# Splitting the first of seven second-layer products in the 768-row parts of a one-core attention and mixture-of-experts kernel

## Chip, cores and metric

The kernel runs on one core of one Trainium2 chip. The metric is device microseconds (us) of one execution; lower is better. All arithmetic of the part in question is in 32-bit floats.

## What is computed

The block adds two things to its input `x` (8 sequences of 1024 tokens, 512 features): an attention layer on the normalised input, and then a mixture of 8 expert networks on the normalised sum. Each token goes to its two likeliest experts, with at most 160 tokens of each sequence per expert, so every expert has 1280 rows. The change touches only the second of the two matrix products of an expert:

```python
h = jax.nn.relu(jnp.einsum('enc,ech->enh', buf, W1) + b1[:, None, :])
y = jnp.einsum('enh,ehc->enc', h, W2) + b2[:, None, :]
```

`buf` holds the gathered rows (512 features), the hidden width is 2048, and `y` has 512 features again. The rows of `y` are multiplied by the probability of their expert and added into the output.

## The kernel before

**The order of the work.** Attention comes first; its last matmuls start at 1248 us. Then come 16 parts, two per expert: an even part of 768 rows (`nh = 3`) and an odd part of 512 rows (`nh = 2`). Each part runs a first layer (class `Hidden`, `layer1`, L1239 to L1321, matmuls at L1258) in eight steps, and then a second layer. The second layer of part 0 is `layer2` (L1361) alone. The seven later even parts go through `layer2_six` (L1545); the odd parts through `layer2_quad` (L1607). The kernel is recorded in a manual schedule: TensorE (PE), VectorE (DVE), ScalarE (ACT) and SyncE (SP) each execute their instructions in the order in which the program calls them. A generator called with `some(1, g)` places its next piece at that point of all the queues.

**Seven products.** Both layers are multiplied by a 2x2 block scheme with seven products in place of eight (Strassen's, in Winograd's form): sums of blocks of both operands are formed on DVE, seven block products run on PE, and further sums give the result. The hidden rows lie in a tile `hid` with seven operand blocks for each of eight column steps, `hid[:, q, k, :]`, for operands k = 0 to 6; the matching blocks of W2 and their sums are in `w2_tiles`. The second-layer product number n takes operand block and weight block as listed in `Second.OPERANDS` (L1444): product 5, for instance, takes operand block 4 and weight block 3.

**A 768-row part** has three blocks of 128 rows in each half. Blocks 0 and 1 are the pair; block 2 is the third block.

- The third block is a generator, `extra = layer2(i, 2, hid)` (L1549). Each of its seven products is eight matmuls of 128x128 by 256 columns (L1372). The first of them starts the accumulator `top`, copied to `y11` at L1384; the second accumulator `mid` comes with the next. Its pieces are placed between the products of the pair by `some(1, extra)`.
- For the pair, product 1 is plain: `pair_product` (L1536), sixteen matmuls of 256 columns (L1540) into one bank, copied to `y11` of both blocks by ACT at L1564.
- The other six products of the pair, in the order 5, 6, 2, 3, 7, 4, are themselves split by the same scheme (class `Second`). `both()` (L1474) puts eight DVE sums of 128x512 on the queue: four of weights (L1460) and four of rows (L1471), one of which is made in place, in `hid`. `run(c)` (L1482) issues seven chains of four matmuls of 128 columns (L1491) into three banks u, v and z, and six copies or sums that bring them to the four quarters of `c`:

```python
chain(u, a11, b11, True)
nc.scalar.copy(c11, u)
between()
chain(v, a21, t1, True)
nc.scalar.copy(c21, v)
chain(u, s2, t2, False)
```

Chain 1 needs no sums; chain 2 needs the first weight differences and the in-place row sum, chain 3 the third sums of both. Chain 3 adds into bank u, so it waits for the copy of c11 (L1500). After it come chains 4 to 7, a DVE sum into c11 (L1507), one into c22 (L1512) and one into c12 (L1513), and an ACT copy of c21 (L1515) that may only overwrite c21 once L1512 has read it.

- The sums need rooms. There are two sets of seven rooms (`sets`, L1555): `room`, made of the tiles `xe` and `xe_s` that the first layer is done with, and `other`, made of three `t1` tiles and the tile `xg`. Products take them in turn. The results go to three further rooms: `c5` for product 5 (and 4), `c6` for product 6, and `c` for all others in turn.
- `gate` (ACT, L1331) multiplies rows by their probability, `send` (POOL, an indirect DMA, L1336) adds them into the output. The y tiles come from a pool of five buffers (`yp`); a part uses six.
- `aside` is the preparation of the next part's rows: its first piece issues eight DMAs (`quarters`, SP, L1117) into `hid`, the columns of the pair's block 0 of operand 0; later pieces are DVE transposes (L1187) and sums (L1200 to L1203). SP's next issues are the loads of W1 (L1047).

Of the kernel before, what the change touches and what calls it, by code (L numbers as in the profile page):

```python
# [12 lines left out]
F32 = mybir.dt.float32  # L13
# [4 lines left out]
ALU = mybir.AluOpType  # L18
# [4 lines left out]
P = 128  # L23
# [51 lines left out]
def preln_attn_moe_kernel(  # L75
# [21 lines left out]
    nc = tc.nc  # L97
# [87 lines left out]
    t = xmp.tile([P, NTT, D], F32, name="x_mid").rearrange("p (i t) d -> p i (t d)", i=2)  # L185
    room = [t[:, i, :].rearrange("p (i s) -> p i s", i=2) for i in range(2)]
    for t in (base_first, room[0]):
        nc.gpsimd.iota(
            t, pattern=[[0, 2], [1, S]], base=0, channel_multiplier=0,
# [544 lines left out]
    def some(count, *gens):  # L734

        for gen in gens:
            while count and next(gen, 0) is None:
                count -= 1

    def rest(gen):  # L740
        got = None
        for got in gen:
            pass
        return got
# [283 lines left out]
    TT, STT = nc.vector.tensor_tensor, nc.vector.scalar_tensor_tensor  # L1028
# [3 lines left out]
    pools = {}  # L1032
# [89 lines left out]
    def new_xg():  # L1122
        return pools["gp"].tile([P, D], F32, name="xg", bufs=1)
# [233 lines left out]
    def new_y():  # L1357
        y = pools["yp"].tile([P, D], F32, name="y")
        return y, y[:, :DC], y[:, DC:]
# [79 lines left out]
    def split(t, part_of):  # L1439
        return [[part_of(t[:, 4 * k : 4 * k + 4], c) for c in range(2)] for k in range(2)]  # L1440

    class Second:

        OPERANDS = {2: (1, 1), 3: (2, 2), 4: (3, 6), 5: (4, 3), 6: (5, 4), 7: (6, 5)}  # L1444

        def __init__(self, i, hid, which, w_room, a_room):
            part, weight = self.OPERANDS[which]
            self.a = split(hid, lambda t, c: t[:, :, part, c * P : (c + 1) * P])
# [75 lines left out]
    two = range(2)  # L1524

    def as_pair(t):
        return t.rearrange("p (c n) -> p c n", n=P)

    def add_to(ys, parts):
        for b in two:  # L1530
            TT(as_pair(ys[b]), as_pair(ys[b]), parts[b], ALU.add)

    def of(ps, b):
        return ps[:, b * DC : (b + 1) * DC]

    def pair_product(i, hid, ps, part, weight, first, last, blocks=two):  # L1536
        ws = w2_tiles[chunks[i][0]]
        for b in blocks:
            for k in range(NHQ):
                nc.tensor.matmul(  # L1540
                    of(ps, b), lhsT=hid[:, k, part, b * P : (b + 1) * P], rhs=ws[weight][:, k, :],
                    start=first and k == 0, stop=last and k == NHQ - 1, skip_group_check=True,
                )

    def layer2_six(i, hid, aside, mix_next):  # L1545

        e = chunks[i][0]
        b2_b = b2_tiles[e]
        extra = layer2(i, 2, hid)  # L1549
        room = units(pools["xep"].tile([P, NCH, 2, HALF], F32, name="xe"), 6)  # L1550
        room += units(pools["xep"].tile([P, 3, 2, HALF], F32, name="xe_s"), 4)
        other = [
            u for _ in range(3) for u in units(pools["t1p"].tile([P, 4, 2, P], F32, name="t1"), 2)
        ] + units(new_xg(), 1)
        sets = [(room[:4], room[4:7]), (other[:4], other[4:7])]  # L1555
        c, c5, c6 = room[7:]
        second = {w: Second(i, hid, w, *sets[n % 2]) for n, w in enumerate((5, 6, 2, 3, 7, 4))}
        gate, send = zip(*(outputs(i, b) for b in two))
        second[5].both()
        top = pools["ps_p"].tile([P, 512], F32, name="ps_p")  # L1560
        y1, y11, y12 = zip(*(new_y() for _ in two))
        pair_product(i, hid, top, 0, 0, True, True)
        for b in two:
            nc.scalar.copy(y11[b], of(top, b))  # L1564
        second[6].both()
        five = second[5].run(c5)
        second[2].both()
        six = second[6].run(c6)
        for b in two:
            TT(six[b], six[b], as_pair(y11[b]), ALU.add)  # L1570
        TT(c5, c5, c6, ALU.add)
        some(1, extra)
        second[3].both()
        some(1, extra)
        add_to(y11, second[2].run(c))
        second[7].both()
        three = second[3].run(c)
        for b in two:
            TT(as_pair(y12[b]), five[b], three[b], ALU.add)
            TT(y1[b], y1[b], b2_b, ALU.add)  # L1580
        some(1, extra)
        for b in two:
            gate[b](0, y1[b])
            send[b](0, y1[b])
        second[4].both()
        some(1, extra)
        seven = second[7].run(c)
        y2, y21, y22 = zip(*(new_y() for _ in two))
        for b in two:
            TT(as_pair(y22[b]), five[b], seven[b], ALU.add)  # L1590
        TT(c6, c6, c, ALU.add)
        some(1, aside)
        four = second[4].run(c5, lambda: some(2, aside), lambda: some(1, aside))
        for b in two:
            TT(as_pair(y21[b]), six[b], four[b], ALU.add)
            TT(y2[b], y2[b], b2_b, ALU.add)
        some(1, aside)
        some(1, extra)
        for b in two:
            gate[b](1, y2[b])  # L1600
            send[b](1, y2[b])
        some(1, aside)
        some(1, extra)
        mix_next()
        rest(extra)
# [96 lines left out]
    def experts(ending):  # L1702
        pools["hp"] = to_end.pool("hp", 1, **right)
        pools["ps_tr"] = to_end.pool("ps_tr", 2, space=PSUM, reuse_waits="tile")
        pools["ps_p"] = to_end.pool("ps_p", 6, space=PSUM, reuse_waits="tile")
        box = first_parts
        mixes = loads = iter(())
        for i, (e, j0, nh) in enumerate(chunks):
            parts, box = box[0], [None]
            hid = pools["hp"].tile([P, NHQ, 7, HALF], F32, name="hid")  # L1710
            tiles, second, early_sums = None, None, iter(())
            if nh == 2:
                second = seconds(i, hid)
                early_sums = itertools.chain(second[0][5].weights(), second[0][2].weights())
            ahead = rows_ahead(i + 1) if i and i + 1 < len(chunks) else iter(())
            for q in range(NHQ):
                if i or q != NHQ - AHEAD - 1:
                    load_ahead(i * NHQ + q + AHEAD)
                some(3, loads)
                if q + 1 < NHQ:  # L1720
                    mix_w1(i, q + 1)
                if i and q > 1:
                    some(4 if q < 4 else 8, mixes)
                next(ahead, None)
                if 2 < q < 7:
                    some(2, early_sums)
                beside = [ending] if i or q < NHQ - 2 else [mixes] * (q + 3 - NHQ)
                tiles = layer1(Hidden(i, q, parts, hid, beside), tiles, q == NHQ - 1)
                if i == 0 and q == NHQ // 2:
                    rest(ending)  # L1730
                    to_router.close()
                    for name, bufs in (("w2p", 1), ("yp", 5), ("bp", 1)):
                        pools[name] = to_end.pool(name, bufs, reuse_waits="tile", **left)
                    load_ahead(NHQ - 1)
                    load_b2(0)
                    rest(load_w2(0))
                    mixes = mix_w2(0)
            rest(mixes)
            rest(ahead)
            room = [hid[:, 4 * h : 4 * h + 4, 0, :P] for h in range(2)] if i and nh > 2 else None  # L1740
            aside = start(gather(i + 1, room), box) if i + 1 < len(chunks) else iter(())
            if i == 0:

                aside = itertools.chain(behind(8, later_on(find_rows, 1)), aside)

            def mix_next():
                if i + 1 < len(chunks):
                    mix_w1(i + 1, 0)

            if i and nh > 2:  # L1750
                layer2_six(i, hid, aside, mix_next)
            elif i:
                layer2_quad(i, hid, second, aside, mix_next)
            else:
                for block in range(nh):
                    if block == nh - 1:
                        mix_next()
                    for _ in layer2(i, block, hid):
                        next(aside, None)
            rest(aside)  # L1760
            if i % 2 and e + 1 < E:
                load_b2(e + 1)
                loads = load_w2(e + 1)
                mixes = mix_w2(e + 1)
# [25 lines left out]
    for n in range(NCK):  # L1790
        more, late = n + 1 < NCK, last is not None
        b, c = divmod(n, NCH)
# [212 lines left out]
```

## Time and profile before

| what | us |
|---|---|
| median of 3 runs | 3158.21 (3156.91 to 3158.54) |
| the profiled execution | 3160.96 |
| its span, first to last instruction | 3159.2 |
| ACT busy in the span | 1686.1 (53%) |
| weight loads on PE busy in the span | 2149.6 (68%) |
| L1540 matmuls on PE, all parts (512 and 480 rows) | 113.4 and 106.0 |
| ACT copies at L1564 | 14, of 372 to 379 ns |

How to read it: the page gives for each engine the time in which it was busy, its share of the span and its number of instructions. The trace can be asked for the rows of one engine in a stretch of time; such a row gives the start in us from the start of the span, the length in us, the engine, the line of the kernel, the operation with output and input tiles, the shape and the number of equal instructions merged into it, and in brackets the idle time ahead of it with what ended it. Consecutive matmuls overlap at their ends, so the price of one is the distance from start to start, not its length. A 32-bit matmul of the program stands as two rows of the trace: the sixteen of `pair_product` are "x32". A further view gives the busy time of every engine and the granted TensorE clock in a stretch.

### The profile page before, as it was taken

What the parts mean: (1) busy time and instruction counts of PE and PEld (TensorE: products, weight loads), DVE (VectorE), ACT (ScalarE), POOL (GpSimd) and SP (SyncE); (2) the same over time, 40 slices, a digit from 0 to 9 for tenths busy, and PEclk for the clock granted to TensorE, in tenths of its full rate; (3) what the DMA queues carried; (4) which work ended last, traced back from release to release, by engine and by line L of the source; (5) the groups of instructions that cost most, each with busy time, mean ns of one, the idle gap of its engine ahead of it and who ended that gap; (6) DMA issues with size and microseconds to landing.
All of it is one profiled execution on the core that took longest, in us unless ns stands there. A gap on an engine that the chain in (4) does not pass through costs nothing.

```text
span 3159.2 us, 53457 instructions
## 1 busy us (share of the span) xinstructions
PE 3085.4 (98%) x20422; PEld 2149.6 (68%) x20422; DVE 2393.9 (76%) x4962; ACT 1686.1 (53%) x2672; POOL 421.3 (13%) x387
## 2 busy tenths in 40 slices
PE   5999999999999999999999999999999999999998
PEld 2454444544444544689699699699698698698697
DVE  8888888888888776738678678677777777777775
ACT  7888888888788885413423423423423423423423
POOL 3000202010101122320110110010110010110110
PEclk9999999999999999999999999999999999999999
DMA  5435454544545352433523523523523523423421
GB/s 168 148 101 167 110 165 133 156 135 147 155 140 161 81 168 63 142 84 96 156 52 92 156 50 99 155 50 99 150 54 102 142 57 105 135 57 108 133 46 22
DMA packets 288559, 358.86 MB, mean 114 GB/s; under 512 B 28376, under 2 KB 199088, under 8 KB 276272
## 3 DMA queue, kind: packets, MB, share of 16 engines
q1 hardware_dynamic: 264944, 312.20, 33.4%
q0 software_dynamic: 22912, 43.22, 7.5%
q8 instruction: 162, 2.65, 0.4%
q14 instruction: 93, 0.76, 0.1%
q10 hardware_dynamic: 448, 0.02, 0.0%
HBM read 207.02 MB, written 81.22 MB: 91 GB/s over the span
## 4 chain that ended last, share of the span: by engine, by line
PE 75%; ACT 12%; DVE 7%; DMA 3%; issue 2%; SPq 0%; POOLq 0%; POOL 0%; ACTq 0%; DVEq 0%
PE ps_p L1258 30%; PE ps_p L1491 13%; PE ps_s L688 8%; PE ps_p L1372 8%; PE ps_p L1540 7%; PE av L722 7%; ACT e L708 6%; ACT qk_c L598 1%; DMA xn_d<-xn 1%; ACT t_r L449 1%; PE ps_s L216 1%; ACT qk_r L449 1%; ACT L598 1%; DMA qk<-qk_r 1%; ACT L1908 1%
## 5 line engine op out<-in xcount | busy, mean ns | idle before, releaser
L688 PE MATMUL ps_s<-qk 64*128 64x512 f32 (+3 forms) x3072 | 584.6, 503 | 31.3 <-ACT e L708 13.7
L708 ACT ACTIVATE e<-ps_s 128x1024 f32<-128x1024 f32 (+1 forms) x640 | 554.4, 944 | 73.4 <-PE ps_s L702 45.3
L722 PE MATMUL av<-e,v 128*64 128x512 f32 (+3 forms) x3072 | 509.5, 488 | 0.0
L688 PEld LDWEIGHTS ps_s<-qk 64*128 64x128 f32 x3072 | 261.1, 188 | 219.1 <-ACT e L708 105.9
L722 PEld LDWEIGHTS av<-e,v 128*64 128x64 f32 x3072 | 206.0, 137 | 278.9 <-issue 258.5
L1258 PE MATMUL ps_p<-xe,w 128*128 128x256 f32 (+1 forms) x1024 | 317.6, 433 | 1.1 <-issue 1.1
L1258 PE MATMUL ps_p<-xe_s,t 128*128 128x256 f32 (+1 forms) x1024 | 317.7, 433 | 0.0
L1258 PE MATMUL ps_p<-xe,t 128*128 128x256 f32 (+1 forms) x1024 | 317.7, 433 | 0.0
L1336 POOL DMA_INDIRECT out_dram<-y,slots x80 | 127.6, 1595 | 1237.2 <-ACT y L1331 956.8
L773 POOL DMA_INDIRECT slot_d<-token,slot x128 | 153.6, 1200 | 1026.2 <-issue 627.2
L1258 PEld LDWEIGHTS ps_p<-xe_s,t 128*128 128x128 f32 x1024 | 194.4, 190 | 81.4 <-issue 0.8
L1258 PEld LDWEIGHTS ps_p<-xe,t 128*128 128x128 f32 x1024 | 194.2, 190 | 80.4 <-issue 0.4
L1258 PEld LDWEIGHTS ps_p<-xe,w 128*128 128x128 f32 x1024 | 193.7, 190 | 79.4 <-issue 1.2
L1301 DVE TENSOR_TENSOR hid<-hid 128x256 f32<-128x256 f32 (+1 forms) x128 | 63.5, 496 | 199.3 <-ACT hid L1299 199.1
L1258 PE MATMUL ps_p<-xe_s,w 128*128 128x256 f32 (+1 forms) x512 | 158.9, 433 | 0.6 <-ACT p L1274 0.6
L1372 PE MATMUL ps_p<-w,hid 128*128 128x256 f32 x640 | 142.9, 379 | 0.0
L1491 PE MATMUL ps_p<-w,hid 128*128 128x128 f32 x1104 | 141.8, 275 | 0.0
L702 PEld LDWEIGHTS <-keys_b 64*128 64x128 bf16 x1536 | 78.7, 95 | 91.1 <-issue 72.4
L730 DVE TENSOR_SCALAR av_sb<-av,inv_o 128x512 f32<-128x512 f32 x128 | 94.4, 746 | 57.7 <-PE av L722 57.6
L1491 PEld LDWEIGHTS ps_p<-w,hid 128*128 128x128 f32 x1104 | 135.3, 192 | 1.9
L1372 PEld LDWEIGHTS ps_p<-w,hid 128*128 128x128 f32 x640 | 121.1, 190 | 16.4
L1268 ACT COPY hid<-ps_p 128x256 f32<-128x256 f32 (+1 forms) x128 | 53.9, 421 | 139.4 <-PE ps_p L1258 127.4
(314 smaller groups left out, 5502.3 us busy)
## 6 DMA issues: line engine op xcount, KB each, us to landing
w<-in_L_ffn_W_dram SPq DMA_DIRECT2D x256, 256.0 KB, 3.5
w<-in_L_ffn_W_dram SPq DMA_DIRECT2D x64, 512.0 KB, 6.6
qk<-qk_c SPq DMA_DIRECT2D x124, 256.0 KB, 4.6
qk<-qk_r SPq DMA_DIRECT2D x120, 256.0 KB, 5.2
qk_base<-base_d SPq DMA_DIRECT2D x28, 1024.0 KB, 6.5
xn_d<-xn SPq DMA_DIRECT2D x72, 256.0 KB, 2.4
rows_d<-xg SPq DMA_DIRECT2D x70, 256.0 KB, 2.1
x_mid<-in_L_attn_x_dram SPq DMA_DIRECT2D x16, 1024.0 KB, 9.9
```

What stands on the lines that cost most here:

```text
L688: nc.tensor.matmul(ps[:, a, at : at + w], lhsT=pair[r, 1, kb * P : (kb + 1) * P], rhs=pair[r, 0, q0 : q0 + w], start=at == 0, stop=not own ...
L702: nc.tensor.matmul(out_, lhsT=keys_b[r, part, :], rhs=late, start=False, stop=part == 1, skip_group_check=True,)
L708: nc.scalar.activation(e, ps[:, :, :n], AF.Exp, scale=UNIT * UNIT / math.sqrt(2 * DH))
L722: nc.tensor.matmul(av[a * 64 : (a + 1) * 64, q0 - 512 * h :], lhsT=vt[:, kb, 2 * pr + a, :], rhs=es[i][:, a, at : at + w], start=kb == 0, ...
L730: nc.vector.tensor_scalar(av_sb, av, inv_o[:, q : q + 1], None, ALU.mult)
L773: queued = nc.gpsimd.indirect_dma_start(out=slot_d[b], out_offset=bass.IndirectOffsetOnAxis(ap=idx, axis=0), in_=src, in_offset=None,)
L1258: nc.tensor.matmul(ps, lhsT=weights[:, k, :], rhs=rows[:, k, :], start=first and k == 0, stop=last and k == 1, skip_group_check=True,)
L1301: TT(g1, g3, h22, ALU.add)
L1336: ins = nc.gpsimd.indirect_dma_start(out=out, out_offset=bass.IndirectOffsetOnAxis(ap=meta[:, e, jj[r], 0:1], axis=0), in_=y, in_offset=No ...
L1372: nc.tensor.matmul(ps, lhsT=hid[:, k, part, cols], rhs=ws[weight][:, k, :], start=first and k == 0, stop=last and k == NHQ - 1, skip_group ...
L1491: nc.tensor.matmul(ps, lhsT=left[:, k, :], rhs=right[:, k, :], start=first and k == 0, stop=k == 3, skip_group_check=True,)
L1540: nc.tensor.matmul(of(ps, b), lhsT=hid[:, k, part, b * P : (b + 1) * P], rhs=ws[weight][:, k, :], start=first and k == 0, stop=last and k ...
```

## The change

Product 1 of the pair in the seven later even parts is split like the other six: `OPERANDS` has an entry for it, `pair_product` is no longer called there, and its result is taken from `c` by two ACT copies to `y11` and by two DVE additions to `c5` and `c6`. The order of the pair's products becomes 5, 6, 1, 2, 3, 7, 4. The two sets of rooms change places, so product 5 now uses the `t1` and `xg` rooms. What the plain product did at the start of the part is done by the third block's first product, which now stands ahead of product 5's chains; the third block's second product stands after product 6, its third after product 2 and its fourth after product 3. The first piece of `aside` moves from after product 7 to ahead of product 3. The function is renamed `layer2_seven`. The y tiles are taken in another order (the third block's first).

```diff
-        OPERANDS = {2: (1, 1), 3: (2, 2), 4: (3, 6), 5: (4, 3), 6: (5, 4), 7: (6, 5)}
+        OPERANDS = {1: (0, 0), 2: (1, 1), 3: (2, 2), 4: (3, 6), 5: (4, 3), 6: (5, 4), 7: (6, 5)}
...
-        sets = [(room[:4], room[4:7]), (other[:4], other[4:7])]
+        sets = [(other[:4], other[4:7]), (room[:4], room[4:7])]
         c, c5, c6 = room[7:]
-        second = {w: Second(i, hid, w, *sets[n % 2]) for n, w in enumerate((5, 6, 2, 3, 7, 4))}
+        second = {w: Second(i, hid, w, *sets[n % 2]) for n, w in enumerate((5, 6, 1, 2, 3, 7, 4))}
         gate, send = zip(*(outputs(i, b) for b in two))
         second[5].both()
-        top = pools["ps_p"].tile([P, 512], F32, name="ps_p")
-        y1, y11, y12 = zip(*(new_y() for _ in two))
-        pair_product(i, hid, top, 0, 0, True, True)
-        for b in two:
-            nc.scalar.copy(y11[b], of(top, b))
+        some(1, extra)
         second[6].both()
         five = second[5].run(c5)
-        second[2].both()
+        second[1].both()
         six = second[6].run(c6)
-        for b in two:
-            TT(six[b], six[b], as_pair(y11[b]), ALU.add)
         TT(c5, c5, c6, ALU.add)
         some(1, extra)
+        second[2].both()
+        one = second[1].run(c)
+        y1, y11, y12 = zip(*(new_y() for _ in two))
+        for b in two:
+            nc.scalar.copy(as_pair(y11[b]), one[b])
+        for t in (c5, c6):
+            TT(t, t, c, ALU.add)
         second[3].both()
+        add_to(y11, second[2].run(c))
         some(1, extra)
-        add_to(y11, second[2].run(c))
         second[7].both()
+        some(1, aside)
         three = second[3].run(c)
...
         second[4].both()
-        some(1, extra)
         seven = second[7].run(c)
...
         TT(c6, c6, c, ALU.add)
-        some(1, aside)
         four = second[4].run(c5, lambda: some(2, aside), lambda: some(1, aside))
```

More of the change, by code (lines that the diff above doesn't have):

```diff
@@ L1543, in pair_product, with layer2_seven @@
                 )
-    def layer2_six(i, hid, aside, mix_next):
+    def layer2_seven(i, hid, aside, mix_next):
         e = chunks[i][0]
@@ L1750, in experts @@
             if i and nh > 2:
-                layer2_six(i, hid, aside, mix_next)
+                layer2_seven(i, hid, aside, mix_next)
             elif i:
```

## The prediction

> **What bounds the kernel now.** I read the page first: PE is busy almost throughout, so only what PE issues or waits for can move the end.
>
> ```profile
> PE 3085.4 (98%) x20422; PEld 2149.6 (68%) x20422; DVE 2393.9 (76%) x4962; ACT 1686.1 (53%) x2672; POOL 421.3 (13%) x387
> ```
>
> A share of the whole span mixes attention with the parts. So I next took one changed stage, the second layer of the third part, as busy time by engine (PE, weight loads, DVE, ACT, POOL, then the granted clock):
>
> ```profile
> 1573.90:1642.60 68.70, 68.70 (x481) 64.94 (x480) 54.71 (x104) 15.29 (x45) 7.34 (x5) 1.00 0.18 32
> ```
>
> The reader is to see that PE fills the stage, and that DVE has only 14 us to spare in it. Then PE's rows in order of time, start first, length second:
>
> ```profile
> 1573.89 7.07 PE L1540 MATMUL ps_p<-w,hid 128*128 128x256 f32 x32
> 1580.79 1.05 PE L1491 MATMUL ps_p<-w,hid 128*128 128x128 f32 x8
> 1581.68 1.06 PE L1491 MATMUL ps_p<-xe,hid 128*128 128x128 f32 x8
> 1582.58 1.06 PE L1491 MATMUL ps_p<-xe 128*128 128x128 f32 x8
> ...
> 1588.85 1.16 PE L1491 MATMUL ps_p<-t,t 128*128 128x128 f32 x8
> 1589.85 1.06 PE L1491 MATMUL ps_p<-w_t,hid 128*128 128x128 f32 x8
> ```
>
> Starts follow each other without a gap, but for one: the chain at 1588.85 takes 1.00 to its successor, the others 0.89 (0.11 lost). Last, what DVE and ACT do meanwhile:
>
> ```profile
> 1577.91 1.29 DVE L1460 TENSOR_TENSOR xe<-w 128x512 f32<-128x512 f32 x2
> 1579.11 0.69 DVE L1471 TENSOR_TENSOR xe<-hid 128x512 f32<-128x512 f32 x1
> 1579.84 0.69 DVE L1471 TENSOR_TENSOR hid<-hid 128x512 f32<-128x512 f32 x1
> ...
> 1581.05 0.68 DVE L1471 TENSOR_TENSOR xe<-hid 128x512 f32<-128x512 f32 x1
> ...
> 1582.85 1.29 DVE L1460 TENSOR_TENSOR t<-w_t 128x512 f32<-128x512 f32 x2
> ...
> 1587.99 0.28 DVE L1512 TENSOR_TENSOR xe_s<-xe_s 128x128 f32<-128x128 f32 x1
> ```
>
> ```profile
> 1588.37 0.27 ACT L1515 COPY xe_s<-ps_p 128x128 f32<-128x128 f32 x1 [2.64 <-DVE xe_s L1512]
> 1588.53 0.27 ACT L1500 COPY xe_s<-ps_p 128x128 f32<-128x128 f32 x1
> ```
>
> The reader is to see that DVE makes product 5's sums only from 1577.91, 4 us after PE has entered the stage, and product 6's right behind. The plain product, 6.9 us of PE work that needs no sums, covers just that time.
>
> **PE's work.** The plain product: 1580.79 - 1573.89 = 6.90 us. A chain of four 128-column matmuls is one "x8" row, 0.893 us from start to start (1580.79 to 1582.58 is two). A split product is seven: 6.25 us. So each part saves 0.65 us of issue, 0.65 x 7 = 4.6 us in all. That is the whole gain: the scheme removes an eighth of the multiplications, but narrower matmuls give part of it back (0.223 us for 128 columns against 0.431 for 256).
>
> **The first gap.** The third block's first product replaces the plain one as cover. It has eight matmuls instead of sixteen: half of 6.90, 3.45 us. Chain 1 of product 5 then starts at 1577.34 and ends at 1578.24. Chain 2 needs the in-place sum in `hid`, DVE's fourth instruction, at 1579.84 + 0.69 = 1580.53. Neither starts earlier in the changed order: all eight sums still stand behind the first layer's last sum (L1304, 1577.43), which hangs on PE's last first-layer matmul. With 0.1 to 0.2 us for the signal PE stands still some 2.4 us, then 0.3 more until chain 3's sum is there (1581.05 + 0.68 = 1581.73).
>
> Product 5 then ends near 1586.4 and product 6 does its chains 1 and 2, to 1588.2. Its chain 3 waits for the ACT copy L1500, which stands behind L1515 of product 5, which waits for DVE's L1512, which stands behind all eight sums of product 6. That queue is the one of before, instruction by instruction, so it lets chain 3 go at the same moment: 1588.53 + 0.27, and PE at 1588.95 (1589.85 less 0.893). Here the two programs stand at the same place of product 6 at the same time, but the new one has done 3.45 us of PE work less. **The first phase costs exactly that: 3.45 us a part**, however its gap divides. The DVE rooms exchanged (`xe` for `t1`) do not matter: sums into either take 0.68 to 0.69.
>
> **The second gap.** From 1588.95: five chains of product 6 (4.47), the third block's second product (3.45), product 1 (6.25), to 1603.12. Product 1 leaves its result in `c`; product 2 writes `c` too, and between them DVE now adds all of `c` to `c5` and to `c6`. The additions need the last quarter, copied by ACT 0.20 after the last chain (in product 2 of before, the last chain ends at 1606.58 and L1515 starts at 1606.78), 0.27 long: 1603.59. Two additions of 512 at 0.60 start to start, the second 0.69 long: from 1603.62 to 1604.91. Only then may L1500 of product 2 overwrite c11: 1605.0 to 1605.27, and PE's chain 3 goes at 1605.42. Chains 1 and 2 of product 2 end at 1604.91. **Gap 0.5 us.** Bounds: 0, if chains 1 and 2 cover it, and 0.9, if the two copies to `y11` go at the 0.72 of a 512-wide ACT row and still hold ACT. I take 0.5, nearest to the chain of rows.
>
> **The rest costs nothing, with these covers.**
> - DVE gains one set of sums (4.95), three quarter sums (0.6) and a net 0.45 (two additions of 512 for two of 256): 6.0 us, 54.7 to 60.7 of about 72. No later product waits: the tightest, product 4, uses its in-place sum at about 1630.3 and has it at about 1626.5. With that cover gone, its lag would be paid in full by PE.
> - SP: the eight row DMAs into `hid` (1575.84 before) now wait until product 1 has read operand 0, about 1600, and SP's W1 loads behind them slip from 1579.5 to about 1604. The rows are wanted by the transposes near 1633, that W1 tile near 1650; landing takes 2 to 5 us. Cover 25 us and more.
> - POOL: the pair's first sends go about 4 us later. The last y tile of a part reuses the first sent one. By the distance of the two sends before (1617.76 to 1623.37, the second waits for the first's landing) it is free at about 1627.3 and written at 1629.9. Cover 2.6 us.
>
> **Sum.** A part: -0.65 + 3.45 + 0.5 = +3.3 us. Seven parts: +23.2. The profiled execution's 3160.96 (span 3159.2 and 1.76 around it) becomes 3184.2. It lies 2.75 above the median of the runs shown, 3158.21; on that scale I forecast **3181.4**.
>
> **The clock.** One row bears on the new gap. From 830.9 to 835.2 PE was idle but for two short groups of transposes (waits of 1.01, 1.28 and 1.01 us), and then:
>
> ```profile
> 835.10:838.60 3.50, 3.43 (x32) 1.14 (x32) 1.21 (x3) 1.59 (x2) 0.00 (x0) 0.66 0.32 124
> ```
>
> The granted clock fell to 0.66 on average, about 3.4 us at half, a loss of 1.7 us. Single waits of PE of 1.00 us (ahead of 531.4) and 1.51 us (ahead of 912.4) left it at 1.00. My gap (2.4 us, a chain of 0.9, then 0.3) lies between the two; I take no fall, since a full chain of matmuls stands in it. If it falls, 0.65 of the 1.7 is hidden by the wait for L1500, so +1.05 a part, 7.4 in all.
>
> The Trainium skill, "TensorE: Matmul & The Clock Gate", section "Why this matters for your kernels", speaks against gaps like mine: idle gaps over about 3 us between bursts of matmuls cost the full clock. By that rule a gap of 2.4 us is still free and the sum stays +23.2; by the row, in which no single wait was over 1.3 us and the clock fell all the same, short work between waits does not protect, and the sum would be +30.6. Where the two differ the row counts.
>
> **The rivals.**
> 1. *Cover enough* (not slower). DVE has the in-place sum by 1578.24, 2.3 us earlier than the row says, so product 5 never waits. The point is chain 2's start. Then the part keeps -0.65, or -0.15 with the second gap: -4.6 to -1, time 3153.6 to 3157. For it: DVE idles 1.48 us ahead of 1575.71. Against: its queue is in order, and the sums stand behind what it idles for. 0.04.
> 2. *Clock*: +23.2 + 7.4, time 3188.8. For: the row above. Against: a chain in between. 0.12.
> 3. *DVE becomes the bound* later in the part: one more wait like the second (0.5) in each, 3.5 us, time 3184.9. For: 6 us more DVE work. Against: covers of about 4 us. 0.12.
> 4. *No second gap*: 2.8 x 7 = 19.6, time 3177.8. 0.12.
>
> The forecast with its own small errors has 0.60. The range takes in rivals 2 to 4 and the bounds of the gaps: 2.3 us a part (first phase 0.5 less, no second gap) gives 3174.3, the clock 3188.8, and 1.6 for spread between runs: 3173 to 3190. A measurement tells 0.2% (6.3 us) from no change: rival 1 lies within it, all others are slower. Faster 0.01, same 0.04, slower 0.95.
>
> **What would show it.** In the profile after: PE idle about 2.4 us ahead of product 5's second chain, seven times, ended by DVE's L1471; product 6's third chain still 15.1 us after the stage begins; a 0.5 us wait in product 2's third chain, ended by ACT L1500; the stage 72.0 us long instead of 68.7; no new wait at the next part's first layer. I am wrong if the first gap is missing, if the granted clock falls in these stages, or if the odd parts change.

## The result, and the profile after

| what | us |
|---|---|
| median before, 6 runs | 3158.58 (3156.91 to 3160.61) |
| median after, 6 runs | 3184.68 (3179.86 to 3189.14) |
| ratio | 1.0082, 95% interval 1.0069 to 1.0095 |
| span of the profiled execution after | 3181.9 |

The kernel became 26.1 us slower; 23.2 had been forecast, which as a median is 3181.4 against 3184.7 measured. The page after, first the line of busy time and then the granted clock, which shows nothing at this scale:

```profile
span 3181.9 us, 53961 instructions
...
PE 3091.7 (97%) x20590; PEld 2161.3 (68%) x20590; DVE 2435.8 (77%) x5039; ACT 1696.4 (53%) x2707; POOL 426.2 (13%) x387
...
PEclk9999999999999999999999999999999999999999
```

PE's busy time grew by only 6 us and the span by 23, so most of what is new is waiting. The view of what PE waited for, from 1500 us to the end (what it waited for; us in total, times, longest):

```profile
PE ps_p L1491 <- DVE hid L1471: 15.3, 7, 2.2
PE ps_p L1491 <- ACT xe_s L1500: 2.4, 8, 0.5
PE ps_p L1540 <- DVE y L1659: 0.8, 1, 0.8
```

The first line was not there before: seven waits of 2.2 us, one in each changed part, ended by the row sum in `hid`. The last line is the only one that this view had before. Where the time went is best told by the length of a stage, from the start of the first second-layer matmul of a part to the start of the next part's first L1258 row. Of the stages from the third part on, these are the changed ones:

| part | 3rd | 5th | 7th | 9th | 11th | 13th | 15th |
|---|---|---|---|---|---|---|---|
| before | 68.72 | 68.71 | 68.72 | 68.72 | 68.72 | 68.72 | 68.72 |
| after | 72.93 | 72.63 | 72.55 | 72.56 | 72.45 | 72.05 | 72.51 |

They sum to 26.6 us more. From the third part on, all other stages are equal to 0.02 us (first layers 72.24 and 48.35, odd second layers 46.05), except the last of all, which is 0.3 longer. In the profiled execution after, the third part began its stage 4.2 us sooner than before (1569.69 against 1573.89), because the attention that precedes it was shorter; a fall of the clock at 836 us, which only the run before has, is a part of that. So the spans differ by only 22.7.

The 13th part is the one in which the clock stayed up. PE's rows there, in order of time:

```profile
2766.01 3.62 PE L1372 MATMUL ps_p<-w,hid 128*128 128x256 f32 x16
2769.47 1.05 PE L1491 MATMUL ps_p<-w,hid 128*128 128x128 f32 x8
2772.70 1.16 PE L1491 MATMUL ps_p<-t,hid 128*128 128x128 f32 x8 [2.18 <-DVE hid L1471]
2774.00 1.13 PE L1491 MATMUL ps_p<-t,t 128*128 128x128 f32 x8
2774.96 1.06 PE L1491 MATMUL ps_p<-w,hid 128*128 128x128 f32 x8
...
2780.97 1.16 PE L1491 MATMUL ps_p<-xe 128*128 128x128 f32 x8 [0.48 <-ACT xe_s L1500]
2781.97 1.06 PE L1491 MATMUL ps_p<-w_t,hid 128*128 128x128 f32 x8
```

The reader is to see the cover of eight matmuls (3.46 us), chain 1, the wait, and then product 6's third chain. A chain without a gap takes 0.89 and its successor starts at 2781.97, so the chain runs from 2781.08, 15.07 us after the stage began. Before it was 1588.95 - 1573.89 = 15.06. The second gap, in the 3rd part, with DVE's additions to `c5` and `c6` ahead of it and the copy that they hold, from the rows of three engines:

```profile
1600.30 1.29 DVE L1573 TENSOR_TENSOR xe_s<-xe_s 128x512 f32<-128x512 f32 x2 [0.90 <-ACT xe_s L1515]
```

```profile
1601.70 0.27 ACT L1500 COPY xe_s<-ps_p 128x128 f32<-128x128 f32 x1 [0.83 <-DVE xe_s L1573]
```

```profile
1600.70 1.06 PE L1491 MATMUL ps_p<-xe,hid 128*128 128x128 f32 x8
1602.02 1.16 PE L1491 MATMUL ps_p<-xe 128*128 128x128 f32 x8 [0.27 <-ACT xe_s L1500]
1603.02 1.06 PE L1491 MATMUL ps_p<-w,hid 128*128 128x128 f32 x8
```

From 1600.70 to 1603.02 two chains take 2.32 instead of 1.79: a gap of 0.53 us.

What the forecast took at nothing is the clock. Windows of the same place in the 3rd and the 13th part (busy PE, weight loads, DVE, ACT, POOL, then the granted clock):

```profile
1576.50:1580.00 3.50, 3.36 (x19) 3.20 (x20) 3.50 (x7) 0.53 (x2) 0.00 (x0) 0.67 0.00 0
...
2772.70:2776.20 3.50, 3.36 (x28) 3.20 (x29) 3.50 (x7) 0.53 (x2) 0.00 (x0) 1.00 0.02 5
```

In the same 3.5 us, PE issued 19 rows in one part and 28 in the other. In the 3rd part the granted clock was 1.00 up to 1577.70, 0.50 for the next 3.41 us and 1.00 after that; the window above catches two thirds of it, hence 0.67. Such a fall came in six of the seven parts, in the first wait or up to 1.3 us behind it.

What sets the seventh apart can be read from when the falls began: 1577.70, 1816.63, 2055.57, 2294.50, 2533.43 and 3011.30. The steps between them are 238.93, and twice that for the last: 70 and 140 times 3.4133, and each fall lasted one such step. So the falls lie on a fixed grid of 3.4133 us. The next step of 238.93 after 2533.43 would be 2772.36, in the 13th part, and the wait there runs from 2770.52 to 2772.70, across that point. The stretch of the grid ahead of the fall in the 3rd part, and the same stretch in the 13th:

```profile
1574.29:1577.70 3.41, 1.18 (x9) 1.02 (x9) 3.38 (x7) 0.33 (x2) 0.00 (x0) 1.00 0.00 0
...
2768.95:2772.36 3.41, 1.57 (x12) 1.30 (x10) 3.27 (x7) 0.64 (x2) 0.00 (x0) 1.00 0.00 0
```

PE was idle for 2.23 us of the first and 1.84 of the second. In the five other parts it was 1.99 to 2.19, and the clock fell. The same wait thus costs the clock or not by where it lies on the grid.

### The profile page after: what moved, and what is told of

Read it like the earlier page. It is cut to its first block, busy times and chain, and to the rows that moved or that the text cites. A ratio compares the mean times of both kernels' runs of the same rounds, so it can differ in the third digit from the quotient of the medians.

```text
span 3181.9 us, 53961 instructions
## 1 busy us (share of the span) xinstructions
PE 3091.7 (97%) x20590; PEld 2161.3 (68%) x20590; DVE 2435.8 (77%) x5039; ACT 1696.4 (53%) x2707; POOL 426.2 (13%) x387
## 4 chain that ended last, share of the span: by engine, by line
PE 74%; ACT 13%; DVE 7%; issue 2%; DMA 2%; SPq 0%; ACTq 0%; POOLq 0%; POOL 0%; DVEq 0%
PE ps_p L1258 30%; PE ps_p L1491 14%; PE ps_s L688 8%; PE av L722 7%; PE ps_p L1372 7%; ACT e L708 6%; PE ps_p L1540 5%; ACT qk_c L598 1%; PE ps_s L216 1%; ACT t_r L449 1%; ACT qk_r L449 1%; DMA qk<-qk_r 1%; DMA xn_d<-xn 1%; ACT L598 1%; ACT L1908 1%
## 5 line engine op out<-in xcount | busy, mean ns | idle before, releaser
L1258 PE MATMUL ps_p<-xe,w 128*128 128x256 f32 (+1 forms) x1024 | 318.6, 434 | 1.1 <-issue 1.1
L1258 PE MATMUL ps_p<-xe,t 128*128 128x256 f32 (+1 forms) x1024 | 318.5, 434 | 0.0
L1258 PE MATMUL ps_p<-xe_s,t 128*128 128x256 f32 (+1 forms) x1024 | 317.7, 433 | 0.0
L1258 PEld LDWEIGHTS ps_p<-xe,t 128*128 128x128 f32 x1024 | 195.0, 191 | 80.9 <-issue 1.6
L1258 PEld LDWEIGHTS ps_p<-xe_s,t 128*128 128x128 f32 x1024 | 194.6, 190 | 81.2 <-issue 0.8
L1258 PEld LDWEIGHTS ps_p<-xe,w 128*128 128x128 f32 x1024 | 194.1, 190 | 79.4 <-issue 1.5
L1258 PE MATMUL ps_p<-xe_s,w 128*128 128x256 f32 (+1 forms) x512 | 158.9, 433 | 0.0
L1491 PE MATMUL ps_p<-w,hid 128*128 128x128 f32 x1216 | 158.1, 277 | 0.0
L1491 PEld LDWEIGHTS ps_p<-w,hid 128*128 128x128 f32 x1216 | 151.2, 194 | 2.3
L1372 PEld LDWEIGHTS ps_p<-w,hid 128*128 128x128 f32 x640 | 120.6, 190 | 17.4
```

The lines of the kernel that those rows point to most:

```text
L1258: nc.tensor.matmul(ps, lhsT=weights[:, k, :], rhs=rows[:, k, :], start=first and k == 0, stop=last and k == 1, skip_group_check=True,)
L1372: nc.tensor.matmul(ps, lhsT=hid[:, k, part, cols], rhs=ws[weight][:, k, :], start=first and k == 0, stop=last and k == NHQ - 1, skip_group ...
L1491: nc.tensor.matmul(ps, lhsT=left[:, k, :], rhs=right[:, k, :], start=first and k == 0, stop=k == 3, skip_group_check=True,)
```

## The experiments

Theory A is the prediction's: the loss is the lost cover ahead of product 5, priced by the end of DVE's queue of sixteen sums, plus the shared room `c`. Rival B: the seventh split itself costs, by 6 us more DVE work a part and by narrower matmuls. Rival C: the clock is the loss. Every kernel was timed or traced beside the kernel before on the same chip; a single run gives a trace but no interval.

### Cover put back

```diff
         second[5].both()
-        some(1, extra)
+        some(2, extra)
         second[6].both()
...
         TT(c5, c5, c6, ALU.add)
-        some(1, extra)
         second[2].both()
```

> The changed kernel, with the third block's first two products ahead of product 5 (6.9 us of work that needs no sums) and none after product 6. Theory A, lost cover: the 2.2 us wait ended by DVE L1471 is gone in all seven parts, product 6's third chain still goes 15.1 us after the stage begins, and the stage is 67.95 us of PE issue + 0.11 + about 0.5 (the wait ahead of product 2's third chain) = 68.6 us against 68.72 before; time about 3157.8, no fall of the clock. Rival B, the seventh split itself is the cost (6 us more DVE work a part, narrower matmuls): the waits move elsewhere and the stage stays near 72, time 3180 and more.

Measured: 3160.03 against 3157.68 before, ratio 1.0005 (0.9995 to 1.0014); every stage 69.05 us. PE no longer waits for L1471; from its waits:

```profile
PE ps_p L1491 <- ACT xe_s L1500: 3.8, 7, 0.5
PE ps_p L1540 <- DVE y L1658: 0.8, 1, 0.8
```

Rival B falls: with all seven products split, 3.0 us a part are gone by moving one third-block product. The second gap, though, was larger than expected: with the third-block product no longer between products 6 and 1, DVE reaches product 1's quarter sums (from 1596.94) only after product 2's eight sums (from 1592.00). From the start of product 2's second chain to that of its fourth, 1597.93 to 1600.53, it takes 2.60 us instead of 1.79, so the gap is 0.81. The other 0.15 or so above the expected 68.6 lies in product 6, whose third chain went 15.24 us after the stage began; the run with seven banks takes that up.

### Lost cover without the split

The kernel before, with the plain product moved behind product 6:

```diff
         second[5].both()
-        top = pools["ps_p"].tile([P, 512], F32, name="ps_p")
-        y1, y11, y12 = zip(*(new_y() for _ in two))
-        pair_product(i, hid, top, 0, 0, True, True)
-        for b in two:
-            nc.scalar.copy(y11[b], of(top, b))
+        some(1, extra)
         second[6].both()
         five = second[5].run(c5)
         second[2].both()
         six = second[6].run(c6)
+        top = pools["ps_p"].tile([P, 512], F32, name="ps_p")
+        y1, y11, y12 = zip(*(new_y() for _ in two))
+        pair_product(i, hid, top, 0, 0, True, True)
+        for b in two:
+            nc.scalar.copy(y11[b], of(top, b))
+        second[3].both()
         for b in two:
             TT(six[b], six[b], as_pair(y11[b]), ALU.add)
         TT(c5, c5, c6, ALU.add)
-        some(1, extra)
-        second[3].both()
-        some(1, extra)
         add_to(y11, second[2].run(c))
+        some(1, extra)
```

> The kernel before, nothing split in addition: the third block's first product as cover ahead of product 5, and the plain product of sixteen matmuls after product 6, in place of two third-block products there. Theory A: the same 2.2 us wait appears without the split; the stage is 68.72 + 3.45 = 72.2 us, and the clock falls in most of these stages, so 3158.6 + 24.2 + 0 to 6, about 3185. Rival B: no more DVE work and no narrower matmul, so 3158.6, no change.

Measured: 3183.70, ratio 1.0084 (1.0067 to 1.0101), as slow as the change, with no further split. Three stages were 72.17 us, the four in which the clock fell 72.61 to 73.05. The waits:

```profile
PE ps_p L1491 <- DVE hid L1471: 15.3, 7, 2.2
PE ps_p L1491 <- ACT xe_s L1500: 1.5, 3, 0.5
```

The first line is that of the changed kernel to the digit. Lost cover makes it, not the split: 72.17 - 68.72 = 3.45.

### The gap filled with idle work

Nine matmuls whose result is never read:

```diff
+        def filler():
+            w = w2_tiles[e][3]
+            spare = pools["ps_p"].tile([P, 512], F32, name="ps_p")[:, :P]
+            for k in range(9):
+                nc.tensor.matmul(
+                    spare, lhsT=hid[:, k % 4, 4, :P], rhs=w[:, k % 4, :P],
+                    start=k == 0, stop=k == 8, skip_group_check=True,
+                )
+
-        five = second[5].run(c5)
+        five = second[5].run(c5, filler)
```

> The changed kernel, with nine matmuls of 128 columns (2.0 us) into a bank that nobody reads between chains 1 and 2 of product 5: PE works through the first gap instead of standing still, all waits for DVE stay as they are. If the falls of the clock come from the idle time and cost 0.4 to 0.9 us in six of seven stages, they vanish: every stage 72.05 us as in the one undisturbed stage, mean clock back to 0.998, time 3158.6 + 7 x 3.33 = about 3182 against 3184.7, and less spread between executions. If the falls come from something else, clock 0.995 and 3184.7. If the gap is not the cause of the slowdown at all, the filler adds its 2.0 us x 7: about 3199.

Measured: 3180.78 (3179.33 to 3181.55), ratio 1.0075 (1.0058 to 1.0091); all seven stages 72.05 or 72.06. The window of the 3rd part's stage shows the clock at 1.00:

```profile
1569.10:1641.20 72.10, 71.03 (x524) 67.40 (x523) 60.67 (x115) 16.67 (x50) 7.74 (x5) 1.00 0.16 32
```

With 2.0 us of added work a part, the seven stages are 3.3 us shorter in sum, and the granted clock was 0.998 in all four runs, against 0.994 to 0.996 in the six of the change. The medians, 3180.8 against 3184.7, point the same way, but they come from different occasions and their ratios' intervals overlap. The stages settle two things. The gap is dead time, for filling it costs nothing. And idle time is what lets the clock fall: without it no stage fell. The clock's share in the profiled execution after is the excess of its stages over 72.05: 0.88 + 0.58 + 0.50 + 0.51 + 0.40 + 0 + 0.46 = 3.3 us of 26.6. Rival C is right in kind and an eighth in size.

### Another order of product 5's sums

`second[5].both()` is replaced by the same eight sums in the order t1, s3, a21, t2, s2, t3, t4, s4, so that the in-place sum a21 comes third instead of fourth.

> The changed kernel, with product 5's eight sums in another order: the in-place row sum, on which chain 2 waits, comes third instead of fourth on DVE. Theory A, that product 6's third chain is released by the end of a DVE queue of sixteen sums and not by the first gap: the first wait shrinks by 0.6 us (2.18 to 1.6), a wait of as much more appears later in products 5 and 6, that chain still goes 15.1 us after the stage begins, and the stage stays 72.05 where the clock stays. Rival, the first gap itself is the price: the stage shrinks by 0.6, to 71.45. For the clock: the idle time is less in one piece, so fewer falls, or the same.

Measured, in a single run: 3184.92. The first wait shrank as expected, a longer wait for product 6's copy of c11 took its place (line numbers of `run` have moved by 15: L1515 here is L1500 of the other kernels, L1506 is the chain, and L1495 is the sum), and the stage was 72.05 in the 13th part, where the clock stayed:

```profile
PE ps_p L1506 <- DVE hid L1495: 11.1, 7, 1.6
PE ps_p L1506 <- ACT xe_s L1515: 3.0, 8, 1.1
...
```

```profile
2773.72 1.16 PE L1506 MATMUL ps_p<-t,hid 128*128 128x128 f32 x8 [1.58 <-DVE hid L1495]
...
2782.59 1.16 PE L1506 MATMUL ps_p<-xe 128*128 128x128 f32 x8 [1.09 <-ACT xe_s L1515]
2783.59 1.06 PE L1506 MATMUL ps_p<-w_t,hid 128*128 128x128 f32 x8
```

0.6 us saved at the first wait (2.18 to 1.58) is 0.6 us waited at the second (0.48 to 1.09), and product 6's third chain again runs from 15.07 us after the stage began (2782.70 - 2767.63): the release that counts is the end of the sixteen sums. The largest line of the view of waits is thus not the thing to shorten by itself. The other six stages were 72.33, so the clock still fell in six of seven, now with waits of 1.6 us.

### A room of its own for product 1

```diff
-        one = second[1].run(c)
+        c1 = hid[:, :4, 4, :P]
+        one = second[1].run(c1)
...
-            TT(t, t, c, ALU.add)
+            TT(t, t, c1, ALU.add)
```

> The changed kernel, with product 1's result in a room of its own; the first gap is left. Theory A (the second gap is the shared room): the 0.5 us ahead of product 2's third chain goes, every stage is 0.5 us shorter, 71.5 where the clock stays and up to 72.4 where it falls, time about 3181. If the two copies to the y tile on ACT hold product 2's first copy instead: stage 72.05 as before this edit.

Measured, in a single run: 3183.39. The wait for L1500 is gone from the view of waits, but the clock fell in all seven stages (71.99 to 72.27; here all seven stretches of the grid held 2.15 to 2.18 us of idle time), so no undisturbed stage showed 71.5. The same room together with the filler:

> The changed kernel with the nine idle-filling matmuls in the first gap and with a room of its own for product 1's result. The clock should stay, as with the filler alone, so the stage shows the second gap by itself: 72.05 - 0.5 = 71.5 us in all seven parts if the shared room makes it, 72.05 if not. Time about 3177.

Measured, in a single run: 3176.67, all seven stages 71.51 or 71.52, clock 0.998. Against 72.05 or 72.06 with the filler alone the shared room costs 0.54 us a part; the two copies to `y11` stay where they were, so they are not what holds product 2.

### Cover and room together

The edits of the first run and of the room run.

> As the run with two third-block products ahead of product 5, and product 1's result in a room of its own (the first quarter of product 5's row operand in the hidden tile, free by then) instead of the room that product 2 writes next. Theory A: the second gap, 0.5 us ahead of product 2's third chain, goes as well; the stage is 67.95 + 0.11 = 68.1 us, 0.65 less than before, time 3158.6 - 4.3 = about 3154.3, below both kernels. If the second gap is held by something else than the shared room: as without the room, 3157.8.

Measured: 3154.72 against 3157.68, ratio 0.9989 (0.9979 to 0.9998); stages 68.23 or 68.24. Of PE's waits in the parts only the line that was there before is left:

```profile
PE ps_p L1540 <- DVE y L1659: 0.8, 1, 0.8
```

This beats both kernels, the one before by 0.48 us a part, 3.4 in all by the stages and 3.0 by the medians. Of PE's 0.65 us less work a part, 0.48 arrive: the stage lies 0.29 above the 67.95 that its matmuls need, and 0.11 of that was there before.

### Third-block product between products 1 and 2

The other way to close the second gap, on top of the cover:

```diff
+        some(1, extra)
         second[3].both()
         add_to(y11, second[2].run(c))
-        some(1, extra)
         second[7].both()
```

> As the run with two third-block products ahead of product 5, and the third block's third product moved from after product 2 to between products 1 and 2 (3.45 us of PE work that needs nothing of the shared room). Theory A: the additions out of the room are over when product 2's third chain comes, so its 0.8 us wait goes without another room; stage 68.24 as with the room of its own, time about 3154.7. If DVE is the bound there, the wait appears in product 3 instead and the stage stays near 69.05, time 3160.

Measured: 3156.38 against 3160.31 before on that chip, ratio 0.9989 (0.9980 to 0.9999); stages 68.23 or 68.24. Order alone, with no new room, does the same.

### Seven banks

Cover and room, with `ps_p` of seven banks and `ps_tr` of one.

> The two third-block products ahead of product 5 and the room of its own, and in addition seven accumulator banks for the products instead of six (one instead of two for the transposes of the routing in the first part). The stage with six banks is 68.24 us, 0.29 over the 67.95 of issue; 0.11 of it stood ahead of product 6's third chain before, and chain 2 of product 6 now waits for the DVE sum that frees product 5's third bank, since the third block holds two. Theory: with seven banks that wait falls back to 0.11 and the stage to 68.05; time 1.3 us below the run with six, about 3153.5, the first part unchanged within 1 us. If it is not the banks: 68.24.

Measured: stages 68.12 to 68.14, but 3155.95 against 3156.70, ratio 0.9996 (0.9987 to 1.0006). With six banks (cover and room) product 6's first chain starts at 1585.27 and takes the 0.89 of a chain, so its second could start at 1586.16; the chain after that starts at 1587.35, so there are 1587.35 - 0.89 - 1586.16 = 0.30 us of gap ahead of the second. With seven, the second follows the first without one, and a gap of 0.11 (1590.27 - 0.89 - 1589.27) stands ahead of the third, where the kernel before has it too:

```profile
1588.36 1.06 PE L1491 MATMUL ps_p<-xe,hid 128*128 128x128 f32 x8
1589.27 1.16 PE L1491 MATMUL ps_p<-xe 128*128 128x128 f32 x8
1590.27 1.06 PE L1491 MATMUL ps_p<-w_t,hid 128*128 128x128 f32 x8
```

So the two banks that the third block holds while products 5 and 6 run cost some 0.11 us a part (stages of 68.23 or 68.24 against 68.12 to 68.14), 0.8 us in all. The expected gain in time did not come, and the first part shows why: from the last transposes of attention to its second layer it takes 86.95 us with the single bank for transposes (1247.42 to 1334.37) against 84.20 before (1249.75 to 1333.95). PE waits there at the routing's transposes (L830) for 3.8 us in place of 0.7. The seventh bank gains 0.8 us and the one taken away costs 2.7.

### The rooms exchanged

The kernel before with its two sets exchanged:

```diff
-        sets = [(room[:4], room[4:7]), (other[:4], other[4:7])]
+        sets = [(other[:4], other[4:7]), (room[:4], room[4:7])]
```

> The kernel before, with the two sets of rooms exchanged and nothing else. All theories: stage 68.72 as before, time 3158 within the spread of 3 us. A longer stage would say that the rooms, and not the cover, cost.

This expectation missed. Measured, in a single run: 3172.45, with 3160.31 before. The stages were 69.39 to 69.43 and the first layers after them 50.0 (50.06 once) instead of 48.35. Together that is 16.5 us; the time shows only 12.1 because this run reached the third part early (1568.68; the profiled run before 1573.89). The wait is DVE's, where the transposes for the next part begin, and PE waits in turn at the next first layer:

```profile
1627.24 2.09 DVE L1187 STREAM_TRANSPOSE xe<-z 128x512 f32<-128x512 f32 x2 [4.93 <-PE ps_p L1491]
```

```profile
PE ps_p L1258 <- ACT hid L1268: 9.7, 7, 1.4
PE ps_p L1372 <- DVE y L1405: 3.0, 7, 0.4
```

With six products and the sets exchanged, the last one, product 4, has its sums in `xe`, which the next part's rows are to enter, so the transposes wait until product 4's matmuls are over at 1627. If that is the mechanism, seven products need the exchange. The changed kernel with the old order of the sets:

> The changed kernel with the two sets of rooms in their old order. In the kernel before, their exchange alone lengthened the stage by 0.7 us and the next first layer by 1.65, since the last product, 4, then sits in the tiles that the next part's rows want. With seven products the old order puts product 4 there, so theory: the same waits appear here (next first layer 50.0 us instead of 48.35, stage 0.7 longer than 72.05 to 72.9), time about 3185 + 7 x 2.3 = 3201. Rival, the exchange cost something else, per set: 3185 or less.

Measured, in a single run: 3204.37. The next first layers were 50.0 (50.06 once) and the stages 72.72 to 73.99 (72.72 and 72.74 in the two parts where the clock stayed), and the lines of the exchange came back:

```profile
PE ps_p L1491 <- DVE hid L1471: 15.6, 7, 2.5
PE ps_p L1258 <- ACT hid L1268: 9.7, 7, 1.4
PE ps_p L1372 <- DVE y L1405: 2.9, 7, 0.4
```

The rooms are not fast or slow; what counts is which set the last product holds. The exchange is worth about 17 us to the change: 5.6 in the seven stages and 11.6 in the seven first layers. The difference of the times, 3204.4 less 3184.7, is larger because this run reached the third part 3.7 us later than the profiled run of the change.

## Why the prediction was right, step by step

- **What bounds the kernel, PE with no wait in the parts:** right. The stages in which the view of waits shows nothing (68.24 with cover and room, 68.12 with seven banks) lie 0.29 and 0.17 above the 67.95 that their matmuls need.
- **PE's work, -0.65 us a part:** right. The stage with cover and room is 0.48 shorter than before, and 0.6 with seven banks.
- **The first phase, +3.45 us whatever its gap divides:** right. The third chain of product 6 went 15.07 us after the stage began, against 15.06. The run with another order of sums moved 0.6 us between two waits and left the stage alone; the run without the split paid the same 3.45. Putting the cover back saved only 3.0, since two smaller waits then grew (0.28 at the shared room, 0.18 at the banks).
- **The second gap, +0.5:** right, 0.53 by the rows and 0.54 by the two filler runs.
- **The rest at nothing:** right in the kernel as it is. DVE was busy for 60.7 us of the undisturbed stage, as worked out, and no later product waited; the next parts began as before.
- **"The DVE rooms exchanged do not matter":** right for the speed of a sum, wrong as a general word. Alone, the exchange costs 16.5 us; in the change it avoids such a loss. The step looked at what a sum in a room takes, not at who wants the room next.
- **The clock, taken at nothing:** wrong. This was rival 2, given 0.12, and it came in six of seven stages. Its price was over-sized: 0.40 to 0.88 us a part in place of 1.05, since part of the slow time lies in waits that are there anyway. It is 3.3 us in the profiled execution, and with it the sum closes: seven undisturbed stages cost 7 x 3.33 = 23.3, the clock 3.3, together the 26.6 by which the stages grew. The step that failed is "since a full chain of matmuls stands in it": the chain stands behind the wait, and the wait, with little beside it, put 1.99 to 2.23 us of idle time into one stretch of 3.41; in two parts (the 11th and the 15th) the clock fell before that chain had begun. The prediction had itself named a fall of the clock in these stages as a sign that it is wrong, and on this point it was.

The undisturbed stage was forecast at 72.0 and is 72.05. That the profiled execution, 3183.67, came so close to the 3184.2 forecast for it is luck: its shorter attention, 4.2 us, hid the clock's 3.3. Rivals 1, 3 and 4 did not come: the first wait and the second gap were there, and no further wait appeared.

The Trainium skill ("TensorE: Matmul & The Clock Gate", section "Why this matters for your kernels") advises against idle gaps over about 3 us between bursts of matmuls. Taken as the prediction took it, that shorter gaps are free, it did not hold here: the clock fell with single waits of 2.2 us, and in another order of sums with waits of 1.6 us. The measurement decides.

## What to carry to other kernels

Work that needs no preparation is worth more than its own time when it stands where another engine prepares: before such a product is split or replaced, measure how long the preparation takes from the stage's start, and keep that much ready work ahead of it. A wait that is one of several behind the same queue cannot be shortened by itself; find the release that all of them share. And where buffers alternate, count the parity: ask which set the last user holds and who comes for it.

## What the runs showed of the hardware

- The granted TensorE clock fell to half for 3.41 us at a time, and the falls in the parts began on a fixed grid of that step. In the changed kernel it fell behind stretches of the grid with 1.99 us of idle time or more and stayed at 1.84; in the run without the split it fell from 2.07 on and stayed up to 1.95. The border is not the same idle time everywhere: in another order of sums it fell six times with 1.71 to 1.72 and stayed once with 1.69. What else counts is not shown.
- Filling idle PE time with matmuls that nobody reads (2.0 us a part) kept the clock at full in all seven stages and made them 3.3 us shorter in sum.
- A split product of 28 matmuls of 128 columns takes 6.25 us against 6.90 for sixteen of 256: 9.4% less, though it has 12.5% fewer multiplications.
